# Perceiver layer with a quantized feed-forward block: transposing the 4-bit and 8-bit activations by DMA, SBUF to SBUF, in place of TensorE

## Chip, core and metric

One Trainium2 chip, one core of it. The metric is the device time of one execution in microseconds (us), as the median of several runs. The profile is of one further execution, taken by the hardware profiler; its times are counted from the start of its span.

## What is computed

Sixteen samples, each with 64 latent rows of 1024 (so 1024 rows, here "tokens", in 8 tiles of 128) and a context of 1024 rows of 1024. Three residual steps, each on a layer-normalized x:

```python
x = x + xattn(layernorm(x), ctx)     # 32 query heads, 8 key/value heads of 32; projections Wq, Wk, Wv, Wo
x = x + attn(layernorm(x))           # self-attention in a sample, rotary positions, no output projection
x = x + ffn(layernorm(x))

def ffn(x):                          # weights are rounded to -1, 0, 1 times their mean magnitude
    xq = int4_quant(x)               # by token: round(x * sqrt(7) / mean|x|), clipped to -8..7
    gate, up = xq @ w_gate.T, xq @ w_up.T          # 1024 -> 2752
    inter = int8_quant(up * relu(gate) ** 2)       # by token: round(127 * x / max|x|)
    return inter @ w_down.T                        # 2752 -> 1024
```

## The kernel before, in words

Nearly all of SBUF is one tensor, `arena`, and each buffer is a place in it given in KB; so profile rows name `arena` for most operands. Small rings of places (`Ring`) play the part of double buffers. The order of the instructions on every engine is the order in which the Python code emits them: the main program runs in `manual_schedule`, and steps that are to fill gaps lie in a list `fillers` from which `fill()` takes the next.

About the first 1560 us are the cross-attention: keys and values of one sample after another, scores, softmax, and beside it the loading and rounding of the feed-forward weights, which go to DRAM as 8-bit floats (`ternary`). Nothing in the change touches that part.

Then comes the self-attention, a loop over the 8 token tiles t (`for t in range(NT)`, class `Tile2`, from L1043). Beside tile t run the steps of the feed-forward block: first `quantize(t - 1)` (L764), the layer norm and 4-bit rounding of the tile before, on DVE, in three pieces, the last of which writes the rounded tile as bf16 into `xq3` (L782; one place for all tiles). At the end of tile t `transpose3(t - 1)` (L788) turns that tile: eight TensorE transposes of 128x128 into a PSUM tile `xqp` (L791), and one ACT copy into `xqT[t - 1]` (L792), eight chunks side by side with the input dimension on the partitions. From tile 4 on, `gate_up(n, t)` steps (L802) for tiles 0 to 3 are emitted between the pieces of the attention: one step is 8 matmuls for gate and 8 for up (L809) of 344 columns, chunk n of 8 of the inner dimension, with `xqT[t]` as the stationary operand and ternary weights moving; ACT's relu (L817), DVE's product (L818) and POOL's (L821) put the result into `inter[t]`. The weights of chunk n + 3 are fetched by `fetch` (L799, two DMAs of 344 KB on SP's queue) when the last tile of chunk n is through.

After the attention loop, 32 gate/up steps for tiles 4 to 7 follow (`for i, (n, t) in enumerate(steps)`), and a table `beside` says what is emitted after which step: `transpose3(7)` after step 6, the three pieces of `quantize8(t)` (L825) for tiles 0 to 3 after every second step from 9, the transposes of tiles 0 and 1 from steps 14 and 22, and `down` of these tiles after steps 20 and 28. `quantize8` on DVE: the row maximum (L831, 3.0 us), a scaling (L837, 1.65 us), the rounding into `q8[t]` as bf16 (L841, 1.6 us), a factor (L843).

`transpose8(t)` (L858) turns the 128x2752 tile in three pieces of 8, 8 and 6 chunks: 22 TensorE transposes (L870; the last, 64 columns wide, L872) into PSUM tiles `qp`, ACT copies into `qTs[t]` (L873, L875), and a clear of the unused half of the last chunk on POOL (L864). `q8` and `qTs` each have two places, by turns (`q_ring`, `qT_ring`).

`down(t, h)` (L879): 22 accumulating matmuls (L883) for one half of the 1024 output columns, `qTs[t]` stationary, down weights moving, into one of two PSUM banks; DVE scales and adds the residual (L892), SP writes 256 KB out (L895). After the 32 steps comes the tail, tiles 2 to 7: `quantize8(t + 2)`, `down(t, 0)`, two pieces of `transpose8(t + 1)`, `down(t, 1)` with the third piece in its middle (`inside`). These lines fix the order of the tail:

```python
for t in range(2, NT):
    if t + 2 < NT:
        for step in quantize8(t + 2):
            step()
    down(t, 0)
    following = transpose8(t + 1) if t + 1 < NT else []
    for step in following[:2]:
        step()
    down(t, 1, following[2] if following else None)
```

SP issues DMAs in the order of emission, and a DMA whose operands are not ready holds all that come after it on SP.

Of the kernel before, what the change touches and what calls it, by code (L numbers as in the profile page):

```python
# [12 lines left out]
BF = mybir.dt.bfloat16  # L13
F8 = mybir.dt.float8e4
AF = mybir.ActivationFunctionType
ALU = mybir.AluOpType
# [4 lines left out]
P = 128  # L21
# [4 lines left out]
NT = B * NQ // P  # L26
KC = DIM // P
HD = 32
KVD = 256
INTER = 2752  # L30
NCH = 8
CW = INTER // NCH
NIC = (INTER + P - 1) // P
LAST = INTER - (NIC - 1) * P
# [6 lines left out]
MAGIC = 12582912.0  # L41
# [8 lines left out]
def kernel(  # L50
# [21 lines left out]
    nc = tc.nc  # L72
# [11 lines left out]
    def t_tile(shape, dtype, name, n=None):  # L84

        turns[0] ^= 1
        n = turns[0] if n is None else n
        return ps_t.tile(shape, dtype, tag=f"t{n}", name=name)

    def m_tile(name):  # L90
        return ps_m.tile([P, 512], F32, tag="m", name=name)
# [4 lines left out]
    def place(kb, shape, dtype=F32):  # L96

        first, n = round(kb * 256), math.prod(shape) * mybir.dt.size(dtype)
        a = arena[:, first : first + (n + 3) // 4]
        if dtype != F32:  # L100
            a = a.bitcast(dtype)
        a = a[:, : math.prod(shape)]
        if len(shape) > 1:
            names = [f"a{i}" for i in range(len(shape))]
            sizes = dict(zip(names[1:], shape[1:]))
            a = a.rearrange(f"p ({' '.join(names)}) -> p {' '.join(names)}", **sizes)
        return a
# [15 lines left out]
    ident_b = const.tile([P, P], BF, name="ident_b")  # L123
# [491 lines left out]
    class Tile2:  # L615
# [131 lines left out]
    xqT = [  # L747
        place(kb, [KC, P], BF)
        for kb in (176, 178, 193.75, 195.75, 168.5, 170.5, 93.9375, 28)
    ]  # L750

    inter = [
        place(kb, [INTER]) for kb in (48, 58.75, 69.5, 80.25, 0, 10.75, 136, 146.75)
    ]
# [1 line left out]
    relu_ring = Ring(45.4375, 192.25)  # L756
    prod_ring = Ring(172.5, 174)
    wds = [place(112 + c if c < 16 else 6 + c, [DIM], F8) for c in range(NIC)]
    q_ring = Ring(157.5, 162.875)
    qT_ring = Ring(48, 59)  # L760
    xq3 = {}
    wbs = {}
# [23 lines left out]
        return [statistics, magnitude, rounded]  # L786

    def transpose3(t):  # L788
        tp = t_tile([P, KC, P], BF, f"xqp_{t}")
        for k in range(KC):  # L790
            nc.tensor.transpose(tp[:, k, :], xq3[t][:, bass.ts(k, P)], ident_b)  # L791
        nc.scalar.copy(xqT[t], tp)  # L792

    def fetch(n):

        wbs[n] = []
        for i in range(2):
            q = wb_ring.next([KC, CW], F8)
            nc.sync.dma_start(q.rearrange("p k o -> p (k o)"), ternary[i][n % NCH])  # L799
            wbs[n].append(q)  # L800
# [22 lines left out]
    cos_down, q8, qTs = {}, {}, {}  # L823

    def quantize8(t):  # L825

        gamma = small.tile([P, 1], F32, tag="gamma", name=f"gamma_{t}")
        rg = small.tile([P, 1], F32, tag="rg", name=f"rg_{t}")

        def magnitude():  # L830
            nc.vector.tensor_reduce(gamma, inter[t], AX.X, ALU.max, apply_absolute_value=True)  # L831
            nc.vector.tensor_scalar_add(rg, gamma, EPS)
            nc.vector.reciprocal(rg, rg)

        def scale():

            nc.vector.tensor_scalar(inter[t], inter[t], 127.0, rg, ALU.mult, ALU.mult)  # L837

        def rounded():
            q8[t] = q_ring.next([INTER], BF)  # L840
            nc.vector.tensor_scalar(q8[t], inter[t], MAGIC, MAGIC, ALU.add, ALU.subtract)  # L841
            co = small.tile([P, 1], F32, tag="co", name=f"co_{t}")
            nc.vector.tensor_scalar(co, gamma, 1.0 / 127.0, wscale[:, 2:3], ALU.mult, ALU.mult)  # L843
            cos_down[t] = co

        return [magnitude, scale, rounded]
# [10 lines left out]

    def transpose8(t):  # L858


        def piece(c0):
            if c0 == 0:
                qTs[t] = qT_ring.next([NIC, P], BF)
                nc.gpsimd.memset(qTs[t][LAST:, NIC - 1, :], 0.0)  # L864
            q, qT = q8[t], qTs[t]
            n = min(8, NIC - c0)
            tp = t_tile([P, 8, P], BF, f"qp_{t}_{c0}")
            full = n if c0 + n < NIC else n - 1
            for c in range(full):
                nc.tensor.transpose(tp[:, c, :], q[:, bass.ts(c0 + c, P)], ident_b)  # L870
            if full < n:
                nc.tensor.transpose(tp[:LAST, full, :], q[:, (NIC - 1) * P :], ident_b)  # L872
            nc.scalar.copy(qT[:, c0 : c0 + full, :], tp[:, :full, :])  # L873
            if full < n:
                nc.scalar.copy(qT[:LAST, NIC - 1, :], tp[:LAST, full, :])  # L875

        return [lambda c0=c0: piece(c0) for c0 in range(0, NIC, 8)]

    def down(t, h, inside=None):  # L879
        cols = bass.ts(h, 512)  # L880
        ps = m_tile(f"d_{t}_{h}")
        for c in range(NIC):
            nc.tensor.matmul(  # L883
                ps,
                lhsT=qTs[t][:, c, :],
                rhs=wds[c][:, cols],
                start=(c == 0),
                stop=(c == NIC - 1),
            )
            if inside and c == NIC // 2:  # L890
                inside()
        nc.vector.scalar_tensor_tensor(  # L892
            xs[t][:, cols], ps, cos_down[t], xs[t][:, cols], ALU.mult, ALU.add
        )
        nc.sync.dma_start(out[bass.ts(t, P), cols], xs[t][:, cols])  # L895
# [9 lines left out]
    with tc.manual_schedule():  # L905
# [33 lines left out]
        for n in range(2 * B):  # L939
# [21 lines left out]
            following = Unit(n + 1, *tiles[(n + 1) // 2]) if n + 1 < 2 * B else None  # L961
# [81 lines left out]
        for t in range(NT):  # L1043
# [43 lines left out]
            if t:  # L1087
                transpose3(t - 1)
# [10 lines left out]
        beside = {9 + 2 * i: step for i, step in enumerate(sum(map(quantize8, range(4)), []))}  # L1099
        beside[0] = lambda: (pieces[1](), fetch_down())  # L1100
        beside[2] = pieces[2]
        beside[6] = lambda: transpose3(NT - 1)
        for t in range(2):
            for i, step in enumerate(transpose8(t)):
                beside[14 + 8 * t + 2 * i] = step
            beside[20 + 8 * t] = lambda t=t: (down(t, 0), down(t, 1))
        more = None
        for i, (n, t) in enumerate(steps):
# [8 lines left out]
                beside[i]()  # L1117
            if t == NT - 1 and n + 3 < 2 * NCH:
                fetch(n + 3)
        for step in transpose8(2):  # L1120
            step()
        for t in range(2, NT):
            if t + 2 < NT:
                for step in quantize8(t + 2):
                    step()
            down(t, 0)
            following = transpose8(t + 1) if t + 1 < NT else []
            for step in following[:2]:
                step()
            down(t, 1, following[2] if following else None)  # L1130


def _rope_constants():
# [66 lines left out]
```

## Time and profile before

| | |
|---|---|
| time of 3 runs, median (lowest to highest) | 1936.94 us (1934.74 to 1937.29) |
| the profiled execution's own time | 1937.88 us |
| its span, first to last instruction | 1936.1 us |
| granted TensorE clock, mean | 0.997 |
| busy: PE, DVE, ACT, POOL | 98%, 60%, 46%, 43% |
| xqp transposes on PE (L791) | 64 |
| qp transposes on PE (L870, L872) | 168 + 8 |
| ACT copies of them, 128x1024 | 1012 ns each |
| DMAs in the last 140 us | weights 344 KB, 2048 + 640 + 64 KB for down, outputs 256 KB |

How to read the profile: PE is TensorE, DVE the VectorE, ACT the ScalarE, POOL GpSimd, SP the queue that issues nearly all DMAs. A busy PE row says that matmuls were in flight, not how dense they were. The chain of work that ended last is followed back from the last instruction: each line is a start in us, a duration in us, the engine, the tile that is written (or the line's output) and the line, with the number of instructions merged. "issue" is time for which the profile shows no wait. DMA rows give the size in KB and the median us from issue to landing.

### The profile page before, as it was taken

How to read it: one execution, taken by the hardware profiler on the slowest of the kernel's cores; microseconds unless marked ns; L12 is line 12 of the kernel's file. 1: busy time of each engine (PE TensorE's matmuls, PEld its weight loads, DVE VectorE, ACT ScalarE, POOL GpSimd, SP SyncE). 2: the span in 40 equal slices, each digit the busy share in tenths (PEclk: the TensorE clock that was granted, in tenths of full speed). 3: DMA queues.
4: the chain of work that ended last, by engine and by line, in shares of the span. 5: the costliest groups of instructions: out<-in, count | busy, mean ns of one | idle time of the engine just before them, and what ended most of it. 6: DMA issues, size and time to landing. Idle time of an engine off the chain costs nothing.

```text
span 1936.1 us, 27466 instructions
## 1 busy us (share of the span) xinstructions
PE 1906.5 (98%) x11632; PEld 1112.1 (57%) x11632; DVE 1162.8 (60%) x1336; ACT 893.5 (46%) x972; POOL 835.9 (43%) x411
## 2 busy tenths in 40 slices
PE   8999999999999999999999999999899999999999
PEld 5445566566556656656665565564346464666654
DVE  3012777777677767767767676777424245665564
ACT  1243665666566666666656666543101022333221
POOL 1000466456446546645654565466302423444420
PEclk9999999999999999999999999999999999999999
DMA  8224344353343342343343333314011000122201
GB/s 333 73 88 170 103 169 141 126 174 110 118 166 110 120 172 97 123 164 110 128 146 125 113 110 129 119 55 166 8 48 44 0 30 1 31 74 89 85 23 55
DMA packets 47946, 205.52 MB, mean 106 GB/s; under 512 B 7056, under 2 KB 16208, under 8 KB 42832
## 3 DMA queue, kind: packets, MB, share of 16 engines
q1 hardware_dynamic: 40528, 184.77, 27.4%
q10 hardware_dynamic: 7296, 19.01, 2.9%
q8 instruction: 91, 1.49, 0.3%
q14 instruction: 31, 0.25, 0.0%
HBM read 190.98 MB, written 12.78 MB: 105 GB/s over the span
## 4 chain that ended last, share of the span: by engine, by line
PE 83%; DVE 9%; ACT 3%; DMA 3%; issue 1%; POOL 0%; ACTq 0%; DVEq 0%; POOLq 0%
PE k L225 19%; PE v L311 18%; PE q L225 11%; PE t L430 6%; PE wo L225 5%; PE o L491 5%; PE gu L809 4%; PE d L883 4%; DVE arena L475 4%; PE g L809 3%; DMA tops<-arena 2%; DVE arena L449 2%; ACT arena L476 1%; PE v L589 1%; ACT arena L442 1%
## 5 line engine op out<-in xcount | busy, mean ns | idle before, releaser
L482 POOL TENSOR_TENSOR arena<-arena 128x1024 f32<-128x1024 f32 x192 | 574.3, 2991 | 24.9 <-ACT arena L476 9.9
L225 PE MATMUL k<-arena 128*128 128x512 f32 x1056 | 472.2, 600 | 0.0
L311 PE MATMUL v<-arena 128*128 128x256 f32 x1984 | 460.5, 385 | 0.0
L311 PEld LDWEIGHTS v<-arena 128*128 128x128 f32 x1984 | 367.0, 190 | 90.1 <-issue 45.1
L475 DVE TENSOR_TENSOR arena<-arena 128x2048 f32<-128x2048 f32 x128 | 364.0, 2882 | 0.0
L479 POOL TENSOR_TENSOR arena<-arena 128x1024 f32<-128x1024 f32 x32 | 77.6, 2426 | 650.9 <-ACT arena L476 449.7
L449 DVE TENSOR_TENSOR arena<-t,arena 128x512 f32<-128x512 f32 x384 | 262.3, 689 | 151.7 <-ACT arena L442 99.7
L225 PEld LDWEIGHTS k<-arena 128*128 128x128 f32 x1056 | 195.9, 190 | 242.1 <-issue 236.0
L476 ACT ACTIVATE arena<-arena 128x2048 f32<-128x2048 f32 x128 | 244.8, 1912 | 177.2 <-DVE arena L475 177.2
L442 ACT COPY arena<-t 128x1024 f32<-128x1024 f32 x256 | 248.7, 1012 | 167.0 <-DMA tops<-arena 89.6
L225 PE MATMUL q<-arena 128*128 128x512 f32 x512 | 225.4, 596 | 0.6 <-ACT arena L262 0.6
L446 DVE TENSOR_REDUCE arena<-t 128x512 f32<-128x1024 f32 x64 | 78.0, 1224 | 215.3 <-PE t L430 120.2
L225 PEld LDWEIGHTS q<-arena 128*128 128x128 f32 x512 | 95.3, 190 | 115.9 <-issue 113.7
L430 PE MATMUL t<-arena 32*128 32x256 f32 x2048 | 146.7, 400 | 4.1 <-DVE arena L446 4.1
L430 PEld LDWEIGHTS t<-arena 32*128 32x128 f32 x2048 | 92.5, 184 | 68.2 <-issue 47.6
L491 PE MATMUL o<-arena 128*32 128x256 f32 x2048 | 125.5, 384 | 6.1 <-ACT arena L476 6.1
L809 PEld LDWEIGHTS <-arena 128*128 128x128 bf16 x1024 | 97.6, 97 | 55.0 <-issue 5.0
L821 POOL TENSOR_TENSOR arena<-arena 128x344 f32<-128x344 f32 x64 | 70.8, 1108 | 104.8 <-DVE arena L818 95.5
L225 PE MATMUL wo<-arena 128*128 128x512 f32 x256 | 114.9, 604 | 0.0
L318 ACT COPY arena<-v 128x256 f32<-128x256 f32 x124 | 45.8, 369 | 117.9 <-DVE arena L461 90.4
L491 PEld LDWEIGHTS o<-arena 128*32 128x32 f32 x2048 | 59.8, 110 | 63.6 <-issue 17.6
L508 DVE RECIPROCAL arena<-o 128x256 f32<-128x256 f32 x32 | 56.2, 1755 | 64.9 <-PE o L501 64.7
(129 smaller groups left out, 1559.4 us busy)
## 6 DMA issues: line engine op xcount, KB each, us to landing
arena<-in_ctxT SPq DMA_DIRECT2D x31, 2048.0 KB, 9.0
arena<-in_wg SPq DMA_DIRECT2D x32, 688.0 KB, 4.2
arena<-in_wu SPq DMA_DIRECT2D x32, 688.0 KB, 4.2
arena<-in_wd SPq DMA_DIRECT2D x32, 688.0 KB, 4.2
arena<-tops ACTq DMA_DIRECT2D x32, 512.0 KB, 4.0
arena<-ternary SPq DMA_DIRECT2D x32, 344.0 KB, 3.6
ternary<-arena SPq DMA_DIRECT2D x48, 172.0 KB, 1.9
arena<-in_x SPq DMA_DIRECT2D x16, 512.0 KB, 9.9
```

The lines of the kernel that those rows point to most:

```text
L225: nc.tensor.matmul(made[0], lhsT=lhsT(k), rhs=rhs(k), start=(k == 0), stop=(k == KC - 1))
L311: nc.tensor.matmul(ps[:, :KVD], lhsT=ctx_halves[b, h][:, k, bass.ts(kt, P)], rhs=wkvs[:, k, KVD:], start=(k == 0), stop=(k == KC - 1),)
L430: nc.tensor.matmul(ws[jj // 2][:, jj % 2, a, :], lhsT=self.kT[rows, self.g, bass.ts(i * 2 + a, P)], rhs=qa[self.g][rows, bass.ts(self.b, 2 ...
L442: nc.scalar.copy(pt[:, 2 * mine : 2 * mine + 2], ws[mine])
L446: nc.vector.tensor_reduce(m, w.rearrange("p j a c -> p j c a"), AX.X, ALU.max)
L449: nc.vector.tensor_tensor(m, w[:, :, a], m, ALU.max)
L475: nc.vector.tensor_tensor(pt, pt, by.to_broadcast([P, 4, 2, 256]), ALU.subtract)
L476: nc.scalar.activation(pt, pt, AF.Exp)
L479: nc.gpsimd.tensor_tensor(acc, pt[:, :, 0], pt[:, :, 1], ALU.add)
L482: nc.gpsimd.tensor_tensor(acc, acc, pt[:, :, a], ALU.add)
L491: nc.tensor.matmul(self.po[bass.ts(jj, HD), 0:256], lhsT=self.v[:, kt, bass.ts(self.g * 4 + jj, HD)], rhs=self.pts[i][:, jj, a, :], start= ...
L809: nc.tensor.matmul(ps[:, :CW], lhsT=xqT[t][:, k, :], rhs=wbs[n][i][:, k, :], start=(k == 0), stop=(k == KC - 1),)
```

## The change

Both transposes become one DMA for each token tile, issued on SP with the transpose done on the way from SBUF to SBUF. `transpose3(t)` is one DMA from `xq3[t]` to `xqT[t]`, 128x1024 bf16. `transpose8(t)` is one DMA from `q8[t]` to `qTs[t]`; since it moves whole chunks, `q8[t]` gets 22 x 128 = 2816 columns and POOL clears its last 64 in `rounded`, in place of the clear in `qTs[t]`. `q_ring`'s second place moves up by 0.125 KB for the longer rows. There are no PSUM tiles `xqp` and `qp` any more and no ACT copies of them; `down` loses its `inside`. In the table `beside`, `transpose8(0)` stands whole after step 14 and `transpose8(1)` after step 22. In the tail, `transpose8(t + 1)` is emitted before `down(t, 0)`.

```diff
-    q_ring = Ring(157.5, 162.875)
+    q_ring = Ring(157.5, 163)
...
     def transpose3(t):
-        tp = t_tile([P, KC, P], BF, f"xqp_{t}")
-        for k in range(KC):
-            nc.tensor.transpose(tp[:, k, :], xq3[t][:, bass.ts(k, P)], ident_b)
-        nc.scalar.copy(xqT[t], tp)
+        nc.sync.dma_start(xqT[t], xq3[t], transpose=True)
...
         def rounded():
-            q8[t] = q_ring.next([INTER], BF)
-            nc.vector.tensor_scalar(q8[t], inter[t], MAGIC, MAGIC, ALU.add, ALU.subtract)
+            q8[t] = q_ring.next([NIC * P], BF)
+            nc.gpsimd.memset(q8[t][:, INTER:], 0.0)
+            nc.vector.tensor_scalar(q8[t][:, :INTER], inter[t], MAGIC, MAGIC, ALU.add, ALU.subtract)
...
     def transpose8(t):
-        def piece(c0):
...
-            for c in range(full):
-                nc.tensor.transpose(tp[:, c, :], q[:, bass.ts(c0 + c, P)], ident_b)
...
-            nc.scalar.copy(qT[:, c0 : c0 + full, :], tp[:, :full, :])
...
-        return [lambda c0=c0: piece(c0) for c0 in range(0, NIC, 8)]
-
-    def down(t, h, inside=None):
+        qTs[t] = qT_ring.next([NIC, P], BF)
+        nc.sync.dma_start(qTs[t], q8[t], transpose=True)
+
+    def down(t, h):
...
         for t in range(2):
-            for i, step in enumerate(transpose8(t)):
-                beside[14 + 8 * t + 2 * i] = step
+            beside[14 + 8 * t] = lambda t=t: transpose8(t)
             beside[20 + 8 * t] = lambda t=t: (down(t, 0), down(t, 1))
...
-        for step in transpose8(2):
-            step()
+        transpose8(2)
         for t in range(2, NT):
             if t + 2 < NT:
                 for step in quantize8(t + 2):
                     step()
-            down(t, 0)
-            following = transpose8(t + 1) if t + 1 < NT else []
-            for step in following[:2]:
-                step()
-            down(t, 1, following[2] if following else None)
+            if t + 1 < NT:
+                transpose8(t + 1)
+            for h in range(2):
+                down(t, h)
```

More of the change, by code (lines that the diff above doesn't have):

```diff
@@ L858, in transpose8 @@
     def transpose8(t):
-        def piece(c0):
[L862 to L868, printed above, removed]
-            for c in range(full):
[L870 to L875, printed above, removed]
-        return [lambda c0=c0: piece(c0) for c0 in range(0, NIC, 8)]
-    def down(t, h, inside=None):
+        qTs[t] = qT_ring.next([NIC, P], BF)
+        nc.sync.dma_start(qTs[t], q8[t], transpose=True)
+    def down(t, h):
         cols = bass.ts(h, 512)
@@ L889, in down @@
             )
-            if inside and c == NIC // 2:
-                inside()
         nc.vector.scalar_tensor_tensor(
```

## Prediction, made before the changed kernel was run

> **What bounds the kernel now.** I read the page first, then the chain of work that ended last over the stretch with the transposes (1590 us to the end), then DVE's and SP's timelines there, then the DMA issues. The page:
>
> ```profile
> PE 1906.5 (98%) x11632; PEld 1112.1 (57%) x11632; DVE 1162.8 (60%) x1336; ACT 893.5 (46%) x972; POOL 835.9 (43%) x411
> ```
>
> PE is busy for 98% of the span, so what leaves PE is a candidate gain, but only where PE is the last to arrive. The chain says where. At the end of tile 4 of the second attention (start, duration, what):
>
> ```profile
> 1684.72 0.87 PE w L728 x8
> 1685.59 0.46 PE xqp L791 x8
> 1686.08 1.02 ACT arena L792
> 1687.10 0.04 issue
> 1687.14 2.52 PE gu L809 x16
> ```
>
> Eight transposes cost PE 0.46 us, 57 ns each; here PE also waits 1.02 us for ACT's copy out of PSUM, because the next matmuls read it. The down projection:
>
> ```profile
> 1858.76 7.04 PE g L809 x48
> 1865.81 0.46 PE qp L870 x8
> 1866.27 0.02 issue
> 1866.29 1.02 ACT arena L873
> 1867.31 0.04 issue
> 1867.35 0.44 PE qp L870 x5
> 1867.79 0.17 PE qp L872
> 1867.97 4.86 PE d L883 x22
> 1872.82 0.89 PE qp L870 x16
> 1873.71 2.59 PE d L883 x12
> 1876.31 0.28 PE qp L870 x5
> 1876.58 0.17 PE qp L872
> 1876.76 7.01 PE d L883 x32
> ```
>
> One tile's 44 matmuls take 9.50 us where they run together (1819.53 to 1829.02 in the same view), and the tail advances by 10.95 us a tile (the x16 group of transposes stands at 1872.82, 1883.77, 1894.72, 1905.67, 1916.62). So the 22 transposes cost 1.45 us: 0.89+0.28+0.17 of their own and 0.1 for changing over. PE has no gap; the tail is PE-bound. DVE needs, per tile, about 8.2 us there (6.75 of 8-bit quantization, two evictions L892 of 0.75), under 9.50.
>
> **What goes.** Call T3(t) the transpose of the 4-bit tile t, T8(t) of the 8-bit one. T3 leaves PE eight times. T3(0), (2), (4), (5), (7) are on the chain with 0.45 us each: 2.25. T3(3) is the fence above: 0.46 and the wait, 1.55 until L809. T3(1) (1627.74) counts nothing: PE then waits for DVE's L735 to free the PSUM tile until 1629.57 anyway. T3(6) (1766.72) counts nothing: PE stalls later for DVE, whose work on tile 7 starts from POOL's L741, released by PE's L728 before T3(6). Sum 3.8 us.
> T8(0): 0.51+0.45+0.45, T8(1): 0.45 three times, and 0.1 each for the matmuls after the last group (4.80 instead of 4.70): 3.0. T8(2): 1865.81 to 1867.97 with its wait for ACT, 2.16. T8(3) to T8(7): 1867.97 to 1932.33 is 64.4 us for six tiles of 9.50, so 7.4. Sum 12.5 us. ACT's copies (L792, L873, L875) and POOL's small clears (0.20 us each) go too; they count nothing but in the two waits already booked.
>
> **What comes.** Sixteen DMAs on SP's queue: eight of 256 KB, eight of 704 KB (22 blocks of 128x128). No row of before has a transposing DMA, so its time L, from issue to landing, is bounded. The nearest rows, plain DMAs of like size (KB each, us to landing):
>
> ```profile
> arena<-in_wg SPq DMA_DIRECT2D x32, 688.0 KB, 4.2
> arena<-ternary SPq DMA_DIRECT2D x32, 344.0 KB, 3.6
> out<-arena SPq DMA_DIRECT2D x16, 256.0 KB, 2.0
> ```
>
> Low end: the transpose is as fast, 4.2 us for T8 and 2.0 for T3. High end, and the rule against this change: the Trainium skill, "VectorE: DVE Perf Modes", section "The three transpose paths", gives a 128x128 bf16 transpose 390 ns on TensorE and 1309 ns by DMA, and advises TensorE where PSUM will do as destination. The trace puts TensorE's at 57 ns in a run of eight, so the rule's comparison is even worse for the DMA. Charged by the block, T8 is 22 x 1.309 = 28.8 us and T3 10.5 us. But 1309 ns for 32 KB may be mostly the fixed part of any DMA. The skill's "DMA: Bandwidth & Descriptors", section "Latency and other measured facts", gives a large transposing DMA 261 GB/s; the fixed part is not above 2.0 us, in which the last row moves 256 KB. By these, an estimate: T8 720,896 B / 261 GB/s + 2.0 = 4.8 us, T3 3.0 us. I take 4.8 and 3.0: they lie next to the rows. By the block rule the sum would come out some 80 us slower (rivals below), by the rate rule 16 us faster.
>
> **What waits for them.** A transposing DMA starts when DVE has rounded the tile; PE needs it later. The slack, from before's timelines:
> - T3(3): rounded at 1681.08, read by L809 straight after L728 ends, 1685.59: 4.5 us. Tightest of the T3s; L of 3.0 fits. T3(7): rounded 1780.46, read by the tenth gate/up step, near 1789.8: 9.3 us. The others have over 8.
> - T8(0): rounded 1803.75, read near 1818: 14 us. T8(1) is queued on SP behind the two output DMAs of down tile 0, which wait for L892 (ends 1829.8); it is read near 1848: about 18 us.
> - T8(2) is behind the outputs of down tile 1. Call X the end of that tile (1858.76). L892 ends at X+0.8, the output's issue takes 0.33 on SP, so T8(2) starts at X+1.15, and PE comes for it after three gate/up steps, X+7.04: slack 5.9 us. 4.8 fits.
> - T8(3) starts when DVE has rounded it, X+9.25, and is needed at X+16.5: slack 7.3. T8(4) to (7) start 1.2 us after a down tile ends (destination free, output issued) and have the next one's 9.50 us: slack about 8.3.
> What is queued behind: weight fetches L799. The first four now wait for T3(0), about 1599 instead of 1571, and are read at 1656; later ones wait at most for a rounding that is a few us away and are read a chunk or more later. The 2 MB of down weights starts after T3(6), a few us late, and is read 40 us later. DVE's rounding of tile t+2 now waits until T8(t) has read the shared buffer, and rounding of T3(t+1) until T3(t) has; both DMAs land several us before DVE gets there. POOL's eight new clears of 64 columns (about 0.2 us, by L864) wait likewise; the cover is the same, and at L over the slack above they would hold only work behind a late DMA.
> One stall is new: with the 1.45 us gone, DVE's first tail tile is late. It rounds tile 3, quantizes tile 4, and frees the bank of down(2, first half) at 1875.59 = X+16.83, when PE wants it at X+16.54: 0.3 us lost, once; from then on 8.2 against 9.5.
>
> **Sum.** 3.8 + 12.5 - 0.3 = 16.0 us. Against the profiled execution (span 1936.1, 1937.9 with what lies around it) that is 1921.9; the median of the runs is 0.9 lower, so 1936.94 - 16.0 = 1920.9 us.
>
> **Rivals.**
> (1) As summed: L(T8) up to about 6 us, L(T3) under 4.5. 1920.9, between 1918.5 and 1923.5, since some of the 0.45s may be met again by a wait for DVE, and ACT's relief may give a us more. For it: DMA is at a few tenths here, plain rows of this size take 4.2. Chance 0.60.
> (2) Faster, but less: L(T8) of 6 to 11.4 us. T8(2) stalls by L-5.9; from T8(4) on each DMA is released by the down tile two before, so two tiles take 9.5 + 1.5 + L. Counted through, the last down tile ends at X + 1.2 + L + max(57, 41+2L): at L = 8 that is X+66.2, at 10 X+72.2, where before it was X+73.6. With the 6.8 us won ahead of X (3.8 + 3.0), 10 us gives 1936.9 - 6.8 - 1.4 = 1928.7. For it: 704 KB is cut in 22 blocks and the write side is turned, unlike any row. Chance 0.18.
> (3) Slower: the transposing DMA is bound by its blocks, not by bytes. The place is T8 in the tail, double-buffered only; the formula turns from gain to loss at L = 12.7 us, 57 GB/s. At 28.8 us the tail ends at X+128.6, 55 us late; T8(0) stalls 14, T8(1) 11, T3(3) 6, T3(7) 1: 1936.9 - 6.8 + 55 + 32 = 2017 us. Against it: 28.8 us would be 25 GB/s where plain rows of the size move 170. Chance 0.17, anywhere from 1941 up.
> (4) No change within 0.2% (3.9 us, about what a measurement of this kernel can tell): L between 11.4 and 14, or the transposes turn out to be hidden by DVE as T3(1) and T3(6) are. Against the latter: the chain in the tail is PE alone. Chance 0.05. That the change does not do what it says I exclude: PE loses all 240 transposes in the built program's order.
>
> **How the numbers follow.** Faster 0.60 + 0.18 = 0.78, same 0.05, slower 0.17. The range covers (1) and nearly all of (2): 1918.5 to 1932; what is left out is (3), (4) and a little of (2).
>
> **What will show it.** Right: no xqp or qp rows on PE; 704 KB transposes landing in 4 to 6 us; down matmuls x44 back to back, 9.5 us per tile, and the last one ending some 16 us earlier; the stretch from X to the end about 68 us instead of 77. Wrong: PE's L883 waiting for a DMA at the head of each down tile (size of L decides), SP busy for several us in one transposing instruction, T3(3) holding L809, or other transfers (weights, outputs) landing later than 3.6 and 2.0 us because a transpose is in flight.

## The result, and the profile after

| | before | changed |
|---|---|---|
| median of the timed runs | 1936.76 us (4 runs) | 1921.85 us (4 runs, 1916.54 to 1924.66) |
| ratio, with 95% interval | | 0.9917 (0.9903 to 0.9931) |
| profiled execution: time, span | 1937.88, 1936.1 us | 1922.23, 1920.4 us |

By the ratio about 16 us, or 0.8%, faster (13.4 to 18.8 us by its interval); by the two medians 14.9. 1920.9 was forecast. Lines of the changed kernel are a few lower than those of before: L789 is the 4-bit transposing DMA, L859 the 8-bit one, L865 the down matmul (was L883), L872 its eviction (L892), L806 the gate/up matmul (L809).

The page's first line, against the one shown of before: 240 matmuls are gone and 15.4 us of PE's busy time.

```profile
PE 1891.1 (98%) x11392; PEld 1098.6 (57%) x11392; DVE 1162.4 (61%) x1336; ACT 863.7 (45%) x932; POOL 836.7 (44%) x411
```

The rows of the two new DMAs (how long SP is held by one, min/median/max in ns, then the us from issue to landing), first 4-bit, then 8-bit:

```profile
L789 SPq DMA_TRANSPOSE arena<-arena x8: 1232/1232/1335, 1596.0 to 1777.4; - x8
DMA to landing us min/median/max: 3.1/3.1/5.1
```

```profile
L859 SPq DMA_TRANSPOSE arena<-arena x8: 3351/3422/3758, 1801.1 to 1899.0; - x8
DMA to landing us min/median/max: 5.1/5.3/5.5
```

3.1 and 5.3 us, where 3.0 and 4.8 were taken: inside every slack. The chain at the end of attention tile 4 has lost the transposes and the wait for ACT's copy; gate/up follows the attention at once:

```profile
1684.19 0.87 PE w L728 x8
1685.07 2.35 PE gu L806 x16
```

And the down projection from the end of down tile 1 on:

```profile
1852.22 7.06 PE g L806 x48
1859.28 0.03 issue
...
1866.61 1.59 DVE arena L839
1868.20 0.12 DVE co L841
1868.32 0.67 DVE arena L872
1868.99 0.04 issue
1869.03 47.66 PE d L865 x220
```

Down tile 2 stands where the dots are (PE's timeline has it from 1859.28). The chain runs over DVE once, since DVE frees a PSUM bank late; PE's timeline says by how much, and that is the only pause left in the tail:

```profile
1859.11 9.66 PE L865 MATMUL d<-arena 128*128 128x512 fp8e4 x44
1869.03 47.64 PE L865 MATMUL d<-arena 128*128 128x512 fp8e4 x220 [0.27 <-DVE arena L872]
```

Both chains, cut at the same instructions:

| stretch | before, us | after, us | change | forecast |
|---|---|---|---|---|
| start to L693 of attention tile 1, ahead of every transpose | 1592.35 | 1589.46 | -2.89 | none |
| to L629 of tile 2: T3(0) | 10.76 | 10.27 | -0.49 | -0.45 |
| to L629 of tile 3: T3(1) | 26.46 | 26.46 | 0 | 0 |
| to shp of tile 3 | 11.10 | 14.41 | +3.31 | none |
| to L629 of tile 5: T3(2), T3(3) | 48.99 | 46.82 | -2.17 | -2.00 |
| to L629 of tile 7: T3(4), T3(5) | 53.58 | 52.68 | -0.90 | -0.90 |
| to the end of PE's stall on tile 7: T3(6) | 37.76 | 37.78 | +0.02 | 0 |
| to down tile 0: T3(7), T8(0) | 38.53 | 36.56 | -1.97 | -2.0 |
| to down tile 1: T8(1) | 29.74 | 28.29 | -1.45 | -1.45 |
| to down tile 2: T8(2) | 18.70 | 16.55 | -2.15 | -2.16 |
| to the end of the last down tile: T8(3) to T8(7) | 64.36 | 57.41 | -6.95 | -7.1 |

The rows with a transpose sum to 16.06 us, against 16.0. Two rows have none. The lead of 2.89 at the start arises in code that did not change: at 1006 us the two traces stand within 0.02 us (the same L311 group at 1006.09 and 1006.10), at 1120 they are 3.06 apart (1122.60 and 1119.54), and between these before's clock fell (0.85 in the 10 us from 1090, 1.00 in the changed kernel). No instruction of that code differs between the kernels, and the start wanders by more than this from profile to profile (next section), so the lead is not counted to the change. The loss of 3.31 is TensorE's clock. In these rows the time after the window is first the sum, then the busy time of PE, PEld, DVE, ACT and POOL with its instructions, then the granted clock, DMA share and GB/s:

```profile
1624.00:1626.00 2.00, 0.34 (x4) 0.11 (x1) 1.51 (x3) 0.00 (x0) 0.00 (x0) 1.00 0.47 88
1626.00:1628.00 2.00, 1.81 (x46) 1.81 (x48) 0.13 (x1) 0.00 (x0) 1.73 (x1) 0.72 0.24 43
1628.00:1630.00 2.00, 2.00 (x26) 1.60 (x25) 0.66 (x1) 0.00 (x0) 0.63 (x1) 0.50 0.04 8
1630.00:1632.00 2.00, 2.00 (x4) 0.73 (x3) 1.63 (x1) 0.00 (x0) 0.00 (x0) 0.50 0.00 0
1632.00:1634.00 2.00, 2.00 (x4) 0.84 (x3) 0.00 (x0) 0.00 (x0) 0.00 (x0) 0.57 0.00 0
```

After a pause of 1.84 us (PE waits for DVE's L735) the clock is halved for between 6 and 7 us. In before's profile the same pause, with T3(1)'s transposes at its head, left 1.40 us idle and the clock stayed 1.00. So the first profile's gain is the right size partly by two accidents of opposite sign; the experiments ask whether the second is one of chance.

### The profile page after: what moved, and what is told of

It is laid out like the page before. It is cut to its first block, busy times and chain, and to the rows that moved or that the text cites. A ratio compares the mean times of both kernels' runs of the same rounds, so it can differ in the third digit from the quotient of the medians.

```text
span 1920.4 us, 26969 instructions
## 1 busy us (share of the span) xinstructions
PE 1891.1 (98%) x11392; PEld 1098.6 (57%) x11392; DVE 1162.4 (61%) x1336; ACT 863.7 (45%) x932; POOL 836.7 (44%) x411
## 4 chain that ended last, share of the span: by engine, by line
PE 82%; DVE 10%; ACT 3%; DMA 3%; issue 1%; POOL 0%; ACTq 0%; DVEq 0%; POOLq 0%
PE k L225 19%; PE v L311 18%; PE q L225 12%; PE t L430 6%; PE wo L225 5%; PE o L491 5%; DVE arena L475 4%; PE gu L806 4%; PE d L865 3%; PE g L806 3%; DMA tops<-arena 2%; DVE arena L449 2%; ACT arena L476 1%; PE v L589 1%; ACT arena L442 1%
## 5 line engine op out<-in xcount | busy, mean ns | idle before, releaser
L311 PE MATMUL v<-arena 128*128 128x256 f32 x1984 | 460.5, 385 | 0.0
L311 PEld LDWEIGHTS v<-arena 128*128 128x128 f32 x1984 | 367.0, 190 | 90.1 <-issue 45.1
L806 PEld LDWEIGHTS <-arena 128*128 128x128 bf16 x1024 | 98.2, 97 | 54.8 <-issue 5.4
## 6 DMA issues: line engine op xcount, KB each, us to landing
arena<-in_x SPq DMA_DIRECT2D x16, 512.0 KB, 11.1
```

Source lines behind the costliest of these rows:

```text
L311: nc.tensor.matmul(ps[:, :KVD], lhsT=ctx_halves[b, h][:, k, bass.ts(kt, P)], rhs=wkvs[:, k, KVD:], start=(k == 0), stop=(k == KC - 1),)
L806: nc.tensor.matmul(ps[:, :CW], lhsT=xqT[t][:, k, :], rhs=wbs[n][i][:, k, :], start=(k == 0), stop=(k == KC - 1),)
```

## The experiments

The theory: a chain bound by PE, transposes taken from it, DMAs inside their slack. Rivals: the gain comes from elsewhere (ACT, PSUM, the lead at the start); the slack is much larger, or the DMA's price another, than counted. Each kernel below is timed against the kernel before on the same chip: e5 to e8 on one, the others on another. The changed kernel itself was not run on the chip of e5 to e8, so those four are set against it by their ratios.

**The changed kernel again (e1), and once more (e9).** No edit; both on the same chip.

> The changed kernel once more, as the partner of the three others of this chip. Theory (PE's transposes are gone from a PE-bound chain, the DMAs land inside their slack): 16 us under the kernel before, about 1921, where TensorE's clock stays whole; if the clock gate falls to half for some us after the 1.84 us pause at 1624 us of the trace, as in the first profile (3.3 us lost there), up to 3 us more. The rival, that the 2.9 us by which the first profile was already ahead before any transpose belong to the change, expects the same lead in this profile ahead of 1590 us; the theory expects that part to wander by a few us from run to run.

> The changed kernel as the partner of the two others of this chip: about 16 to 17 us under the kernel before, as at first and in the earlier repeat.

Measured: 1919.78 us, ratio 0.9910 (0.9895 to 0.9924), and 1919.29, ratio 0.9913 (0.9897 to 0.9928). Within e1's profile the clock stayed whole at 1624 us (L629 took 2.01 us, not 3.10), in e9's it fell (3.33). The start wanders: the L728 group of attention tile 0, ahead of every transpose, stands at 1570.23 before, at 1567.35 in the first profile, 1567.53 in e1, 1568.27 in e9, and between 1565 and 1573 in the profiles of the other kernels below. So single profiles differ by some us that no edit explains, while the medians of the three sets of timed runs differ from before's by 14.9, 16.5 and 17.8 us.

**The 4-bit transposes alone (e2).** Before, with `transpose3` as in the change:

```diff
     def transpose3(t):
-        tp = t_tile([P, KC, P], BF, f"xqp_{t}")
-        for k in range(KC):
-            nc.tensor.transpose(tp[:, k, :], xq3[t][:, bass.ts(k, P)], ident_b)
-        nc.scalar.copy(xqT[t], tp)
+        nc.sync.dma_start(xqT[t], xq3[t], transpose=True)
```

> Only the 4-bit transposes by DMA, the 8-bit ones on TensorE as before. Theory: 3.8 us faster than before (five times 0.45 and one of 1.55 on PE's chain), 1933, if the clock does not fall after tile 1; if it falls there, about 3 of it are lost and the time is within 1 us of before. A rival that puts the gain into the relief of ACT and PSUM expects more than 6 us here.

Measured: 1933.85, ratio 0.9984 (0.9976 to 0.9993), so 1.4 to 4.6 us faster. As the theory had it, and no room for the rival's 6.

**The 8-bit transposes alone (e3).** The changed kernel with `transpose3` as before.

```diff
     def transpose3(t):
+        if True:
+            tp = t_tile([P, KC, P], BF, f"xqp_{t}")
+            for k in range(KC):
+                nc.tensor.transpose(tp[:, k, :], xq3[t][:, bass.ts(k, P)], ident_b)
+            nc.scalar.copy(xqT[t], tp)
+            return
         nc.sync.dma_start(xqT[t], xq3[t], transpose=True)
```

> Only the 8-bit transposes by DMA, the 4-bit ones on TensorE as before. Theory: 12.2 us faster than before (12.5 less the 0.3 us wait for a PSUM bank), about 1924.6; no fall of the clock at tile 1, since TensorE's eight transposes stand in that pause again.

Measured: 1923.22, ratio 0.9926 (0.9911 to 0.9942), 11.2 to 17.2 us faster; 12.2 were expected. The two parts, 3.1 and 14.3 by ratio, add up to the whole (17.4 by e1's). But the expectation on the clock was wrong: here TensorE's transposes stand in the pause of tile 2, and the clock fell all the same:

```profile
1626.00:1628.00 2.00, 2.00 (x34) 1.29 (x31) 1.09 (x1) 0.00 (x0) 1.25 (x1) 0.84 0.03 8
1628.00:1630.00 2.00, 2.00 (x4) 0.84 (x3) 1.20 (x1) 0.00 (x0) 0.00 (x0) 0.50 0.00 0
1630.00:1632.00 2.00, 2.00 (x5) 0.77 (x4) 0.00 (x0) 0.00 (x0) 0.00 (x0) 0.81 0.00 0
```

**T3(1) back on TensorE (e4).**

```diff
     def transpose3(t):
+        if t == 1:
+            tp = t_tile([P, KC, P], BF, f"xqp_{t}")
+            for k in range(KC):
+                nc.tensor.transpose(tp[:, k, :], xq3[t][:, bass.ts(k, P)], ident_b)
+            nc.scalar.copy(xqT[t], tp)
+            return
         nc.sync.dma_start(xqT[t], xq3[t], transpose=True)
```

> The changed kernel with the 4-bit transpose of tile 1 alone back on TensorE; by the chain it is hidden in a pause in which PE waits for DVE, so its 0.45 us cost nothing. Theory (its removal lets the pause grow from 1.4 to 1.84 us, after which the clock is halved for some us in some runs): 1 to 3 us faster than the changed kernel, with a clock of 1.00 between 1624 and 1640 us, and a narrower spread. Rival (the fall of the clock is chance, or comes from another place): no difference from the changed kernel beyond 0.5 us.

Measured: 1919.40 (1918.03 to 1924.67), ratio 0.9912 (0.9895 to 0.9929), against e1's 1919.78 on the same chip. No difference is seen, as the rival has it; with intervals of 3 us a cost of 1 us or so is not excluded. Over all profiles of this study the clock fell near 1630 us in 8 of 10 without T3(1) on TensorE and in 1 of 3 with it. T3(1) in its place does not prevent the fall (e3); whether it makes it rarer is open.

**The DMA later on SP (e5).** Emission between the halves of a down tile:

```diff
-            if t + 1 < NT:
-                transpose8(t + 1)
-            for h in range(2):
-                down(t, h)
+            down(t, 0)
+            if t + 1 < NT:
+                transpose8(t + 1)
+            down(t, 1)
```

> The changed kernel with the tail's 8-bit transposing DMA emitted between the two halves of a down tile, as the TensorE transposes were, instead of ahead of both. It is then queued on SP behind the first half's output, which waits for DVE. Theory: it starts at about 5.9 us into the 9.5 us tile (4.75 for the half, 0.75 for DVE, 0.4 for SP) and lands 5.3 later, so PE waits about 1.7 us at each of five tiles, 8 us slower than the changed kernel, about 1929. Rival (the place on SP's queue does not matter, the DMA is hidden anyway): same as the changed kernel within 1 us.

Measured: 1936.95, ratio 1.0006 (0.9995 to 1.0017): the whole gain is gone, about 17 us by the ratios against the 8 expected. PE's timeline of the tail (start, busy, and in brackets the idle time ahead with what ended it):

```profile
1864.71 9.66 PE L865 MATMUL d<-arena 128*128 128x512 fp8e4 x44
1880.43 11.35 PE L865 MATMUL d<-arena 128*128 128x512 fp8e4 x44 [6.06 <-DMA arena<-arena]
1893.64 9.67 PE L865 MATMUL d<-arena 128*128 128x512 fp8e4 x44 [1.87 <-DMA arena<-arena]
1905.78 9.67 PE L865 MATMUL d<-arena 128*128 128x512 fp8e4 x44 [2.47 <-DMA arena<-arena]
1917.34 9.67 PE L865 MATMUL d<-arena 128*128 128x512 fp8e4 x44 [1.89 <-DMA arena<-arena]
1928.95 9.67 PE L865 MATMUL d<-arena 128*128 128x512 fp8e4 x44 [1.94 <-DMA arena<-arena]
```

The last four waits, 1.9 to 2.5 us, are the 1.7 foreseen. The first is not. The chain shows what SP stood behind:

```profile
1872.21 1.59 DVE arena L839
1873.80 0.12 DVE co L841
1873.92 0.67 DVE arena L872
1874.61 0.34 SPq L875
...
1875.11 5.27 DMA arena<-arena
1880.38 0.05 issue
1880.43 6.61 PE d L865 x22
```

The eviction L872 of down tile 2's first half comes behind DVE's quantization of tile 4, the output L875 behind it, the transposing DMA behind that. The clock then fell, and tile 3 took 11.35 us instead of 9.66; after the shorter waits it stayed whole:

```profile
1880.00:1890.00 10.00, 9.57 (x37) 4.05 (x38) 2.72 (x4) 0.00 (x0) 0.15 (x1) 0.81 0.17 51
1890.00:1900.00 10.00, 8.13 (x39) 3.53 (x37) 8.02 (x8) 0.00 (x0) 0.15 (x1) 1.00 0.42 92
1900.00:1910.00 10.00, 7.53 (x36) 3.25 (x35) 6.51 (x6) 0.00 (x0) 0.15 (x1) 1.00 0.54 126
```

This profile's execution took 1944.18 us, 7 more than the median of its runs; down tile 2 starts 5.6 us later in it than in the first profile of the changed kernel, which the edit, made in the tail alone, does not explain. From the start of down tile 2 to the end of the last tile it is 73.9 us here and 57.6 there: 16.3 us, the loss that the timed runs show. One place later on SP's queue costs all that the change brings.

**A longer landing: twice (e6) and, with `range(3)`, three times (e7).**

```diff
-        nc.sync.dma_start(qTs[t], q8[t], transpose=True)
+        for _ in range(2):
+            nc.sync.dma_start(qTs[t], q8[t], transpose=True)
```

> The changed kernel with each 8-bit transposing DMA done twice, the second waiting for the first, so that the time from issue to landing is about 10.6 instead of 5.3 us. By the count of the prediction's second rival (last down tile ends at X + 1.2 + L + max(57, 41 + 2L), X the end of down tile 1): X + 74.0 instead of X + 64.5, 9.5 us slower than the changed kernel, about 1931, and a little more if the clock falls in PE's waits of 3 to 6 us. Rival (slack is much larger than counted): no change.

> Each 8-bit transposing DMA done three times in a row, L about 15.9 us. By the same count X + 89.9, 25 us slower than the changed kernel plus 1.5 for tile 0, about 1948, slower than the kernel before; more if the clock falls in PE's waits. With 10.6 and 15.9 us on both sides of 12.7, where the prediction put the point at which the change turns into a loss, the twice-done one should be faster than before and this one slower.

Measured: e6 1935.72, ratio 0.9995 (0.9984 to 1.0005); e7 1967.94, ratio 1.0147 (1.0122 to 1.0172). Both are slower than expected: e6, which was to keep part of the gain, is level with the kernel before, and e7 loses more than its count. e6's tail:

```profile
1860.84 20.85 PE L866 MATMUL d<-arena 128*128 128x512 fp8e4 x88 [4.91 <-DMA arena<-arena]
1884.69 20.85 PE L866 MATMUL d<-arena 128*128 128x512 fp8e4 x88 [3.00 <-DMA arena<-arena]
1907.87 20.85 PE L866 MATMUL d<-arena 128*128 128x512 fp8e4 x88 [2.32 <-DMA arena<-arena]
```

Its waits, 4.91 + 3.00 + 2.32 = 10.2 us, are the 9.5 of the count. But two down tiles take 20.85 us after a wait where 19.16 is their pace: 1.7 us each time, 5.1 in all. The granted clock has the fall, here after the first wait:

```profile
1860.00:1870.00 10.00, 9.16 (x35) 3.87 (x36) 5.60 (x7) 0.00 (x0) 0.15 (x1) 0.83 0.72 134
1870.00:1880.00 10.00, 10.00 (x48) 4.51 (x46) 7.63 (x8) 0.00 (x0) 0.15 (x1) 1.00 0.66 138
```

Waits and clock make 15.3 us, and by the ratios e6 lies 15 to 16.5 us behind the changed kernel. In e7 the waits sum to 32.7 us and seven tiles of 11.1 to 12.3 us instead of 9.66 add 14.2; the count had 26.5 for the waits. There the count also forgot that tile 3's DMAs stand on SP behind tile 2's: SP's six follow one another from 1854.77 to 1884.61. So the change breaks even near a landing of 10.6 us, not 12.7 (a pair also holds SP twice as long as one DMA, which these runs do not part from its landing).

**The price by the block: 22 DMAs (e8).**

```diff
-        nc.sync.dma_start(qTs[t], q8[t], transpose=True)
+        for c in range(NIC):
+            nc.sync.dma_start(qTs[t][:, c, :], q8[t][:, bass.ts(c, P)], transpose=True)
```

> Each 8-bit transpose as 22 transposing DMAs of one 128x128 block, in place of one DMA of 22 blocks. The rule that charges 1309 ns to a block expects 28.8 us a tile and over 1990 us. The theory that 1309 ns is mostly the fixed part of one DMA, which overlaps among DMAs in flight, expects SP's issue to set the pace: 22 x 0.2 to 0.33 us, 5 to 8 us of landing after the last issue included 7 to 9 us a tile, so 2 to 8 us slower than the changed kernel, 1923 to 1930.

Measured: 2063.92, ratio 1.0640 (1.0607 to 1.0673). The expectation failed. SP's row for one block, and a piece of the chain:

```profile
L860 SPq DMA_TRANSPOSE arena<-arena x176: 1095/1182/2172, 1799.0 to 2048.2; - x176
DMA to landing us min/median/max: 2.2/2.3/4.1
```

```profile
1885.18 1.18 SPq L860
1886.36 0.05 issue
1886.46 1.18 SPq L860
1887.64 0.05 issue
1887.73 1.19 SPq L860
```

A transposing DMA of one block holds SP for 1.18 us, one of 8 blocks for 1.23, a plain DMA of 344 KB for 0.32 (L799). From one issue to the next it is 1.28 us, so 22 take 28 us, about what the prediction's rule of 1309 ns a block would ask. The rule's figure is near the price of an instruction of one block; it does not multiply with the blocks of one instruction, where 22 hold SP for 3.42 us.

**Two DMAs of 11 blocks (e11).**

```diff
-        nc.sync.dma_start(qTs[t], q8[t], transpose=True)
+        for c0 in (0, NIC // 2):
+            cs = slice(c0, c0 + NIC // 2)
+            nc.sync.dma_start(qTs[t][:, cs, :], q8[t][:, cs.start * P : cs.stop * P], transpose=True)
```

> Each 8-bit transpose as two transposing DMAs of 11 blocks instead of one of 22. In the run with 22 DMAs of one block SP was held 1.2 us by each, however small; in the changed kernel 1.2 us by 8 blocks and 3.4 by 22. If SP's hold is a fixed 1.2 us or so plus 0.16 us for each block beyond eight, two halves hold SP 2 x 1.7 us and land as late as the one DMA: within 1 us of the changed kernel. If instead the price were by the DMA, a second fixed part in series, the second half would land 2 to 3 us later than the one DMA does, near the slack of 5.9 and 7.3 us of tiles 2 and 3: 1 to 5 us slower.

Measured: 1920.71, ratio 0.9917 (0.9899 to 0.9935), as the changed kernel (e9: 0.9913). One half holds SP for 1.6 us and lands in 3.8; a pair holds it for 3.1, so the second half lands about when the one DMA does. The timed runs alone do not exclude a loss of 1 us or two; PE's tail does: its one pause there is again the 0.27 us for DVE, and none is for a DMA. The first expectation held.

**One more family of transposes (e10).** The softmax shifts of each attention tile, too:

```diff
-            tp = t_tile([P, 8 * P], BF, f"shp2_{self.t}")
-            for c in range(8):
-                nc.tensor.transpose(
-                    tp[:, bass.ts(c, P)],
-                    parts2[self.t % 2][:, c].rearrange("p j k -> p (j k)"),
-                    ident_b,
-                )
             self.sh = sh2_ring.next([2, 2, 256], BF)
-            nc.scalar.copy(self.sh.rearrange("p b g c -> p (b g c)"), tp)
+            nc.sync.dma_start(
+                self.sh.rearrange("p b g c -> p (b g c)").rearrange("p (n q) -> p n q", q=P),
+                parts2[self.t % 2].rearrange("p c j k -> p (c j k)"),
+                transpose=True,
+            )
```

> The changed kernel with one more family of bf16 transposes moved: the eight 128x128 transposes of the softmax shifts in each self-attention tile (rows shp, 0.45 to 0.62 us on PE's chain, and ACT's copy of 1.0 us) become one transposing DMA of 256 KB, which the tile's second scores read one gate/up or query step or more later. If PE's time is what counts wherever a landing of 3.1 us fits behind a step, about 8 x 0.5 = 4 us are won, 1915.5; in tiles 2 and 3, where PE waits for DVE ahead of these transposes and one step of 3.5 us follows, a us more or less. Rival: the DMA follows DVE's chain and is read sooner than T8 and T3 were, so PE waits for its landing where one step of 3.5 us is the only cover, and SP holds it behind fetches that wait for PE; then no gain, or up to 8 x 1.5 = 12 us lost, clock falls included.

Measured: 1918.35, ratio 0.9897 (0.9881 to 0.9913), beside e9's 1919.29 and 0.9913 (0.9897 to 0.9928). The best median of all, but the intervals overlap: against e9 it is 0.9 us by the medians and 3 by the ratios, where 4 were expected. The traces are clearer. From L629 of tile 4 to down tile 0 it is 151.4 us (1663.48 to 1814.86) where e9 takes 153.4 (1661.98 to 1815.34): 0.5 us a tile, as foreseen. PE's waits for these DMAs stay small, all in all

```profile
PE w L657 <- DMA arena<-arena: 2.4, 4, 1.7
```

2.4 us in four waits of eight tiles (longest 1.7, in tile 3 where DVE is last anyway). The rival's loss of up to 12 us is excluded; that the version is faster rests on the trace, 2.0 us in this stretch, and is not shown by the timed runs.

## Why the prediction was right, step by step

- What goes: the chain gave every term of T3 and T8 within 0.2 us (table above), the two zeros (T3(1), T3(6)) included. e2 and e3 confirm the two sums apart, within intervals of 3 and 6 us.
- What comes: 5.3 us for 704 KB and 3.1 for 256 KB, where the rate rule with 2.0 us fixed gave 4.8 and 3.0. The differences, 2.2 us for 458,752 B more, are 209 GB/s, under the 261 that the Trainium skill, "DMA: Bandwidth & Descriptors", section "Latency and other measured facts", gives for a transposing DMA with a non-contiguous middle dimension. The measurement decides; it changed nothing, for every slack was larger: any landing under about 5.9 us for T8 and 4.5 for T3 would have given the same sum. The rule against the change, in the Trainium skill, "VectorE: DVE Perf Modes", section "The three transpose paths" (its advice stands in the page's "Rules for kernel authors"), did not apply, since its price belongs to a DMA instruction (e8) and the change issues one for 8 or 22 blocks.
- Slack: T8(2) was issued at X + 1.26 (1.15 forecast) and landed 0.5 us before PE came; T3(3) was issued at 1680.57, landed at 1683.7, and was read at 1685.07. That these slacks are real, e6 shows by its first wait of 4.91 us (10.6 less 5.9 is 4.7), and e5 by what a later issue costs.
- The new stall on DVE: 0.3 us forecast, 0.27 measured.
- Not foreseen: SP is held for 3.4 us by each 8-bit DMA. It costs nothing here: from 1777 us on PE waits only for DVE, 0.5 and 0.3 us. And the clock: the prediction booked PE's waits at their own length. In rivals (2) and (3) that was wrong: in e6 and e7 the clock adds nearly half as much as the waits themselves (5.1 to 10.2 us, 14.2 to 32.7). The term that was mis-sized is the turning point, 12.7 us: e6 is level with before at 10.6. By an estimate, 5.1 us of lost clock put into the count's 3L give 11.0. In e6 the waits were sized right (10.2 us for 9.5), their price was not.
- Luck: the sum booked no fall of the clock, and one of up to 3.3 us came in 8 of 10 profiles without T3(1) on TensorE, while starts differ by up to 7 us from profile to profile. That the first median lies within 1 us of the forecast is therefore partly chance; the terms in the table are what is shown.
- Open: whether removing T3(1) makes the clock fall more often at that pause (e1, e3, e4).

## What to carry to other kernels

Where TensorE is the chain and a transpose of bf16 data has one DMA's landing of cover (here 3 to 5.5 us), one transposing DMA for a whole tile can give TensorE's time back in full, as here; count a transpose on the chain by its own and by the PSUM copy that the next matmul waits for. Issue it ahead of everything on its queue that waits for the same stage, and do not cut it into DMAs of one block (two halves cost nothing here, 22 pieces 124 us against the kernel before). A wait of PE that such a change adds can cost more than its length: each of those of 2.3 us and more in e6 and e7 was followed by 1.5 to 2.7 us of lost clock, those of 1.9 to 2.5 us in e5 by none.

## What the runs showed of the hardware that was not expected

- SP's time for one transposing DMA: 1.18 us for 1 block of 128x128 bf16, 1.23 for 8, 1.6 for 11, 3.42 for 22 (e8; the 4-bit DMA; e11; the 8-bit DMA); a plain DMA of 344 KB 0.32. Landing: 2.3, 3.1, 3.8, 5.3 us.
- The granted clock fell to 0.50 after pauses of PE of 1.84 us (first profile) and 2.32 us (e6), and each such fall cost some 1.7 to 3.3 us. The Trainium skill, "TensorE: Matmul & The Clock Gate", section "Part 1: The HAM clock gate", puts the fall after an idle window of about 3.4 us; here shorter pauses sufficed, and not in every run. The pause of 1.84 us left the clock whole in e1 and e6, four of 1.87 to 2.47 us did so in e5, and one of 2.03 us ahead of shp in tile 3 did in the profiles of both kernels but not in those of e5 and e11 (0.83 in the 10 us from 1640). What decides between them is open.
- With transposing DMAs in flight among the weight fetches and outputs the medians of these did not rise: 344 KB landed in 3.4 us (3.6 before), 256 KB in 2.0 (2.0).
